# A forward stage whose Haar transform is multiplied into its convolution filters

## The chip, the cores and the metric

The kernel runs on one core of one Trainium2 chip. The metric is device time in microseconds (us) of one execution, as a median of several. Engines are named as in the profile: PE is TensorE's matmul, PEld its weight loads, DVE VectorE, ACT ScalarE, POOL GpSimd, SP SyncE, whose queue issues nearly all DMAs here.

## The reference

Four layers act one after the other on x, float32 of shape (4, 64, 256, 256). Layers 0, 2 and 3 are long convolutions along both image axes with separable filters, plus a bias times the input. Layer 1 goes to 2-D Haar coefficients, mixes channels, shrinks, and goes back.

```python
# layers 0, 2, 3: hx, hy are [256, 64] filters from a small sine network
k = einsum('ijk,imk->ijmk', hx, hy)            # separable, one per channel
y = irfft2(rfft2(x, 512) * rfft2(k, 512) / 512)[:256, :256]   # causal convolution
x = y + x * bias[:, None, None]

# layer 1
f1 = haar2d(x); acc = 0
for i in range(2):
    f4 = einsum('bchw,oc->bohw', f1 * v[i], conv_w[i])
    acc += sign(f4) * relu(abs(f4) - tau[i])
x = haar2d(acc, inverse=True) + x
```

## The kernel before, in words

**Groups and rounds.** The four images form two groups of two. A round is two channels of one group, so each group has 32 rounds, and a round's tile is [128, 8, 256] float32 (1 MB): an image axis is cut into four blocks of 64 rows, and the 128 partitions are two halves of 64.

**Phase A, forward** (`phase_a`, 64 rounds): layer 0 and the forward Haar. A convolution along one axis is a product with a Toeplitz matrix. `load_toeplitz` reads it from DRAM, where each filter was repeated, with a sheared access pattern; `toeplitz` then does 16 matmuls of 64x64 weights for each block row j, four at a time in the four quarters of PE (`TILES`), with 256, 192, 128 and 64 moving columns for k = 0 to 3. The data are the weights, the filter moves, so that each product also transposes. A round has four `rows` pieces (PSUM tiles `a1ps`, emptied by ACT into `ay`, L441) and four `columns` pieces (`a2ps`, emptied by DVE, which adds bias times x in `residual`, L461). The Haar along the free axis is eight levels of sums and differences on POOL (`forward_free`, L341 and L343, 16 instructions a round). The Haar along the other axis is a product with a 64x64 matrix (`product`, PSUM `a3ps`, L305), scaled by row on DVE (L474). `store` writes the coefficients to DRAM (`coef0`, `coef1`).

**Phase B, coefficients** (`phase_b(0)`, `phase_b(1)`, 64 steps for each group): layer 1's middle. A step has two units, one for each i. A unit: mixing on PE (`mix`, L603), times v on DVE (L622), `sign` (L628) and `abs` (L634) on ACT, minus tau (L639) and the thresholded product (L644) on DVE; the sums with the residual's coefficients are POOL's (L659 to L663). `join` on DVE finishes the Haar over the four blocks for the first steps. `abs` writes to PSUM, where it has one buffer. Results go to DRAM (`mixed0`, `mixed1`).

**Phase C, inverse** (`phase_c`, 64 rounds): the inverse Haar on POOL (on DVE for rounds 0 and 1, L384) and PE, then layers 2 and 3 with the same `toeplitz` (`c1r`, `c1c`, `c2r`, `c2c`).

**Order.** All engines run in an order written out by hand. Each phase is a list of pieces (ten for a round of phase A, 18 for one of phase C, three for a unit of phase B), and `beside` interleaves two lists. An operation given to `later` is emitted at the start of the next piece (`flush`). The sequence is: A of group 0; A of group 1 beside B of group 0; the last two rounds of A with the start of C; C of group 0 beside B of group 1; C of group 1. Beside phase B, A's products share a ring of four PSUM tiles, used in pairs (`banks`).

```python
    beside(a[cut_a : -2 * A_PIECES], phase_b(0), 2, 0)
    ...
    main = c_first + a_end[:1] + c[:BLOCKS] + c[mid:C_PIECES] + a_end[1:] + c[BLOCKS:mid] + c[C_PIECES:cut_c]
    beside(main, phase_b(1), len(c_first) + len(a_end) + 2 * BLOCKS, 0)
```

The level buffers of the free-axis Haar (`h2` to `h128`, one buffer each) are shared by the forward and the inverse transform. Group 1 of phase A loads x with one DMA of 1 MB (8 KB a partition), and B of group 0 loads v and tau of both i with one of 1 MB.

## Time and profile before

| | us |
|---|---|
| runs: median of 3 (lowest to highest) | 2605.57 (2600.97 to 2605.86) |
| the profiled execution, own time | 2597.8 |
| its span, first to last instruction | 2595.7 |
| granted TensorE clock, mean over the span | 0.979 |

| stage, by the trace | from, to (us) | PE | DVE | ACT | POOL | DMA share |
|---|---|---|---|---|---|---|
| A of group 0, steady part | 65 to 325 | 99% | 54% | 20% | 87% | 0.73 |
| A of group 1 beside B of group 0, steady part | 520 to 1040 | 82% | 96% | 65% | 91% | 0.94 |
| end of B of group 0 to first product of B of group 1 | 1062 to 1167 | 65% | 47% | 18% | 61% | 0.53 |
| C of group 0 beside B of group 1 | 1235 to 1885 | 95% | 63% | 62% | 66% | 0.87 |
| C of group 1, without its last part | 1885 to 2535 | 99% | 75% | 58% | 91% | 0.65 |

The percentages are busy time over the stage's length. A busy PE is not PE at its peak, since matmuls are pipelined and their ends are modelled. The line number behind L is that of the kernel before; the helper `toeplitz` records all convolutions under L293, so they are told apart by their tiles. Idle time of an engine that is not the bottleneck costs nothing.

### The profile page before, as it was taken

What the parts mean: (1) busy time and instruction counts of PE and PEld (TensorE: products, weight loads), DVE (VectorE), ACT (ScalarE), POOL (GpSimd) and SP (SyncE); (2) the same over time, 40 slices, a digit from 0 to 9 for tenths busy, and PEclk for the clock granted to TensorE, in tenths of its full rate; (3) what the DMA queues carried; (4) which work ended last, traced back from release to release, by engine and by line L of the source; (5) the groups of instructions that cost most, each with busy time, mean ns of one, the idle gap of its engine ahead of it and who ended that gap; (6) DMA issues with size and microseconds to landing.
All of it is one profiled execution on the core that took longest, in us unless ns stands there. A gap on an engine that the chain in (4) does not pass through costs nothing.

```text
span 2595.7 us, 118630 instructions
## 1 busy us (share of the span) xinstructions
PE 2343.0 (90%) x53292; PEld 1915.7 (74%) x53292; DVE 1800.2 (69%) x2049; ACT 1325.6 (51%) x2187; POOL 2025.0 (78%) x2428
## 2 busy tenths in 40 slices
PE   5999999788888888768999999999989999999999
PEld 4887877444444444547777877788889999999998
DVE  2555445799999999646666666666658777777773
ACT  1221112566666666226666665666655655655552
POOL 1898887899999999757657666766679999999991
PEclk8999999899999999979999999999999999999999
DMA  7676897699999999556989888888776666666653
GB/s 209 222 242 231 289 311 281 245 347 317 343 330 328 347 319 335 180 194 214 333 302 315 317 303 302 306 304 311 275 224 203 220 208 215 214 220 207 220 165 113
DMA packets 203678, 685.25 MB, mean 264 GB/s; under 512 B 29289, under 2 KB 30826, under 8 KB 190755
## 3 DMA queue, kind: packets, MB, share of 16 engines
q1 hardware_dynamic: 203171, 677.67, 75.8%
q8 instruction: 418, 6.85, 1.1%
q14 instruction: 89, 0.73, 0.1%
HBM read 427.93 MB, written 249.63 MB: 261 GB/s over the span
## 4 chain that ended last, share of the span: by engine, by line
PE 59%; DVE 13%; DMA 8%; POOL 8%; issue 5%; ACT 3%; SPq 2%; DVEq 0%; ACTq 0%; POOLq 0%
PE c2c L293 10%; PE c2r L293 9%; PE c1c L293 9%; PE c1r L293 9%; PE a1ps L293 6%; PE a2ps L293 5%; PE f L603 4%; PE c0ps L305 4%; DMA v<-in_v 3%; DVE x L622 3%; POOL fw L341 3%; POOL f L343 2%; DVE a L639 2%; DVE m L644 2%; PE a3ps L305 2%
## 5 line engine op out<-in xcount | busy, mean ns | idle before, releaser
L293 PEld LDWEIGHTS a2ps<-toep,ay 64*64 64x64 f32 x8192 | 313.2, 138 | 161.7 <-DVE f L474 85.0
L382 POOL TENSOR_TENSOR i<-i,g 128x16 f32<-128x16 f32 x744 | 398.3, 556 | 27.7 <-ACT g L359 0.6
L293 PE MATMUL a2ps<-toep,ay 64*64 64x128 f32 (+3 forms) x8192 | 360.1, 307 | 50.8 <-DVE f L474 42.4
L603 PE MATMUL f<-ft,mix 64*64 64x512 f32 x2048 | 312.0, 619 | 95.6 <-DVE x L622 80.2
L293 PEld LDWEIGHTS c2c<-toep,ch 64*64 64x64 f32 x8192 | 314.6, 134 | 59.0 <-ACT ch L836 25.9
L293 PEld LDWEIGHTS a1ps<-toep,x 64*64 64x64 f32 x8192 | 293.8, 134 | 83.8 <-issue 43.1
L293 PE MATMUL a1ps<-toep,x 64*64 64x64 f32 (+3 forms) x8192 | 338.8, 300 | 15.3 <-issue 12.3
L293 PEld LDWEIGHTS c1c<-toep,ch 64*64 64x64 f32 x8192 | 313.3, 134 | 51.6 <-ACT ch L836 26.6
L662 POOL TENSOR_TENSOR gt<-m,ft 128x512 f32<-128x512 f32 x128 | 163.6, 1278 | 236.3 <-DVE m L644 230.7
L293 PE MATMUL c1r<-toep,z 64*64 64x128 f32 (+3 forms) x8192 | 324.4, 299 | 21.5 <-issue 11.6
L293 PE MATMUL c2c<-toep,ch 64*64 64x192 f32 (+3 forms) x8192 | 328.7, 300 | 11.8 <-ACT ch L836 8.7
L293 PEld LDWEIGHTS c1r<-toep,z 64*64 64x64 f32 x8192 | 303.9, 134 | 46.6 <-issue 22.2
L293 PE MATMUL c1c<-toep,ch 64*64 64x128 f32 (+3 forms) x8192 | 324.3, 299 | 11.1 <-ACT ch L836 10.4
L382 POOL TENSOR_TENSOR ci<-i,g 128x1024 f32<-128x1024 f32 x124 | 318.2, 2586 | 4.5
L293 PE MATMUL c2r<-toep,cy 64*64 64x128 f32 (+3 forms) x8192 | 318.4, 298 | 2.9 <-issue 2.7
L293 PEld LDWEIGHTS c2r<-toep,cy 64*64 64x64 f32 x8192 | 301.4, 134 | 24.7 <-issue 13.3
L441 ACT COPY ay<-a1ps 128x512 f32<-128x512 f32 x256 | 137.4, 589 | 353.6 <-PE a1ps L293 353.0
L628 ACT ACTIVATE m<-x 128x1024 f32<-128x1024 f32 x194 | 206.3, 1063 | 194.2 <-DVE x L622 87.6
L639 DVE TENSOR_TENSOR a<-a,v 128x1024 f32<-128x1024 f32 x192 | 236.3, 1231 | 49.0 <-ACT a L634 48.9
L836 ACT COPY ch<-c2r 128x512 f32<-128x512 f32 x256 | 137.5, 591 | 247.1 <-PE c2r L293 246.6
L634 ACT ACTIVATE a<-x 128x1024 f32<-128x1024 f32 x194 | 199.6, 1029 | 109.4 <-DVE m L644 109.4
L855 DVE SCALAR_TENSOR_TENSOR cy<-z,bias_sb,c1c 128x512 f32<-128x512 f32 x256 | 176.9, 742 | 109.5 <-PE c1c L293 109.5
(80 smaller groups left out, 3869.2 us busy)
## 6 DMA issues: line engine op xcount, KB each, us to landing
toep<-filt SPq DMA_DIRECT2D x384, 224.0 KB, 5.3
ft<-coef SPq DMA_DIRECT2D x128, 512.0 KB, 7.4
v<-in_v SPq DMA_DIRECT2D x64, 1024.0 KB, 9.4
mixed<-gt SPq DMA_DIRECT2D x128, 512.0 KB, 7.5
g<-mixed SPq DMA_DIRECT2D x256, 256.0 KB, 5.7
x<-in_x SPq DMA_DIRECT2D x128, 256.0 KB, 4.7
coef<-f SPq DMA_DIRECT2D x128, 256.0 KB, 4.2
x<-in_x SPq DMA_DIRECT2D x32, 1024.0 KB, 7.8
```

Of the source, the lines that this page charges most:

```text
L293: nc.tensor.matmul(ps[r][half(c), j % 2, k * ROW :], data[half(r), c, k, bass.ts(j, ROW)], t(r, c)[:, : N - k * ROW], start=k == 0, stop=k ...
L305: nc.tensor.matmul(ps[r][half(c)].rearrange("p h k -> p (h k)"), matrix[half(r)], pairs(r, c).rearrange("p h k -> p (h k)"), start=True, s ...
L341: nc.gpsimd.tensor_tensor(diffs, even, odd, ALU.subtract)
L382: engine.tensor_tensor(to, s, d, op)
L441: later(lambda y=y, ps=ps: nc.scalar.copy(y, ps))
L603: nc.tensor.matmul(un[u]["f4"][half(q), b, :], mixers[0][half(r), bass.ts(i, C)], st[s]["f"][half(r), b], start=True, stop=True, tile_posi ...
L628: nc.scalar.activation(un[u]["m"], un[u]["x"], AF.Sign)
L634: nc.scalar.activation(un[u]["a"], un[u]["x"], AF.Abs)
L639: nc.vector.tensor_tensor(un[u]["a"], un[u]["a"], both(u, "tau"), ALU.subtract)
L662: nc.gpsimd.tensor_tensor(g[:, 0], m[:, 0], st[s]["f"][:, 0], ALU.add)
L836: later(lambda y=y, ps=ps: nc.scalar.copy(y, ps))
L855: nc.vector.scalar_tensor_tensor(to, of, bias_sb[:, at : at + 1], ps, ALU.mult, ALU.add)
```

## The change

It concerns rounds 32 to 63 of phase A, the second group's forward stage.

- `fold` multiplies each round's filters by Haar matrices: `load_hankel` reads the two filters with the opposite shear (2304 B a partition instead of 3584), 32 matmuls of 64x64 by 64 columns form the products, and ACT and DVE copy them to `fold` (one 128x512 copy each). `rows` and `both_axes` then use `fold` in place of the Toeplitz tiles, so their results are already transformed within blocks of 64.
- The bias term becomes a product of its own: `plain` transforms x along one axis (64 matmuls of 64 columns a round, copied by ACT to `u`), and `both_axes` adds `u` times the other Haar matrix times the bias to the same PSUM sum (64 more). DVE's residual and x's long life go.
- `f` comes out of `both_axes` by plain copies, half on ACT, half on DVE. `forward_free`, `product` and the row scaling are not used for these rounds. What is left of the Haar, over the four blocks, is `join_blocks`, five small POOL instructions.
- The end of phase A is shorter: the list `a_end` is gone, and B of group 1 starts four pieces earlier in the main list.
- The second image of the second group comes with its halves swapped, so the mixing has a second, swapped matrix and the inverse Haar writes its PSUM tiles crossed (`haar(..., crossed)`).
- x (group 1) and v with tau (B of group 0) are loaded in two DMAs of 4 KB a partition each. Two buffers of phase B move into a tile of phase A that the second group no longer uses.

```diff
+    def load_hankel(t):
+        rows = ac.tile([P, SPAN - ROW], F32, tag="toep", name=f"hankel_{t}", bufs=4)
+        for r in range(2):
+            start = filt[0].offset + (t % ROUNDS * 2 + r) * REPEATS * SPAN + PERIOD - ROW + 1
+            src = bass.AP(filt[0].tensor, start, [[SPAN + 4, 16], [SPAN + 1, 4], [1, PERIOD + N]])
+            nc.sync.dma_start(rows[half(r), : PERIOD + N], src)
+        return rows
...
-            toeplitz(s["ps"], blocks(s["x"]), filters_x(s["toep"]), j)
+            x_of = (lambda r, c: s["fold"][half(r), c, 0]) if folded(t) else filters_x(s["toep"])
+            toeplitz(s["ps"], blocks(s["x"]), x_of, j)
...
+            if j % 2 and folded(t):
+                plain(t, j)
+
+        def fold(t):
+            s = st[t]
+            s["fold"] = fp.tile([P, 2, 2, N], F32, tag="fold", name=f"fold_{t}", bufs=3)
+            two = banks(f"foldps_{t}")
+            for i in range(2):
+                for k in range(BLOCKS):
+                    for r, c in TILES:
+                        nc.tensor.matmul(
+                            two[r][half(c), i, bass.ts(k, ROW)],
+                            s["hankel"][half(r), i * PERIOD + k * ROW : i * PERIOD + (k + 1) * ROW],
+                            folds_sb[half(r), 0, 0 if i else c], ...
+            def evacuate():
+                nc.scalar.copy(s["fold"][:, 0], two[0])
+                nc.vector.tensor_copy(s["fold"][:, 1], two[1])
+                nc.vector.tensor_scalar(s["bias"], folds_sb[:, 1, 0], pairs_sb[:, at : at + 1], None, ALU.mult)
+            later(evacuate)
+
+        def plain(t, j):
...
+            two = banks(f"u{j}ps_{t}")
+            for i in range(2):
+                for k in range(BLOCKS):
+                    for r, c in TILES:
+                        nc.tensor.matmul(
+                            two[r][half(c), i, bass.ts(k, ROW)],
+                            data[half(r), c, k, bass.ts(j - 1 + i, ROW)],
+                            folds_sb[half(r), 1, r], ...
+            for r, ps in enumerate(two):
+                u = blocks(s["u"])[:, r, j - 1 : j + 1]
+                later(lambda u=u, ps=ps: nc.scalar.copy(u, ps))
+
+        def both_axes(t, j):
...
+            for name in ("y", "u"):
+                data = blocks(s[name])
+                for k in range(BLOCKS):
+                    for r, c in TILES:
+                        q = r ^ c
+                        whole = name == "y"
+                        nc.tensor.matmul(
+                            s["ps2"][c][half(q), j % 2, k * ROW : N if whole else (k + 1) * ROW],
+                            data[half(r), c, k, bass.ts(j, ROW)],
+                            s["fold"][half(r), r, 1, : N - k * ROW] if whole else s["bias"][half(r)], ...
+            if j % 2:
+                for b, ps in enumerate(s["ps2"]):
+                    f = s["f"][:, 2 * (j - 1) + 2 * b : 2 * (j - 1) + 2 * b + 2]
+                    copy = nc.vector.tensor_copy if b else nc.scalar.copy
+                    later(lambda f=f, ps=ps, copy=copy: copy(f, ps))
...
-            if j < middle and 1 < t:
+            if j < half_way and 1 < t <= ROUNDS + 1:
                 run(st[t - 2]["ops"], 3 if j < BLOCKS else 2)
+            if j == 1 and folded(t - 2):
+                join_blocks(t - 2)
+            if j == 3 and folded(t - 2):
+                store(t - 2)
...
-                if 2 < t:
+                if 2 < t <= ROUNDS + 2:
                     product(t - 3, j - BLOCKS)
+                if j == BLOCKS + 1 and folded(t + 1):
+                    fold(t + 1)
...
-    main = c_first + a_end[:1] + c[:BLOCKS] + c[mid:C_PIECES] + a_end[1:] + c[BLOCKS:mid] + c[C_PIECES:cut_c]
-    beside(main, phase_b(1), len(c_first) + len(a_end) + 2 * BLOCKS, 0)
+    main = c_first + c[:BLOCKS] + c[mid:C_PIECES] + c[BLOCKS:mid] + c[C_PIECES:cut_c]
+    beside(main, phase_b(1), len(c_first) + 2 * BLOCKS, 0)
```

## The prediction

> **What bounds the kernel now.** I read the busy time by stage first, because the share of the whole span (PE 90%) mixes stages with different limits. One row per stage; columns: length, then busy time and instructions of PE, PE's weight loads, DVE, ACT and POOL, granted clock, DMA share, GB/s.

> ```profile
> 325.00:448.00 123.00, 111.34 (x2646) 94.75 (x2641) 59.68 (x97) 23.21 (x42) 93.36 (x160) 0.97 0.86 297
> 520.00:1040.00 520.00, 424.93 (x6891) 252.33 (x6887) 496.88 (x508) 337.56 (x419) 472.52 (x518) 0.98 0.94 333
> 1062.00:1167.00 105.00, 68.34 (x1196) 49.83 (x1186) 49.38 (x90) 18.80 (x40) 64.30 (x99) 0.82 0.53 186
> 1235.00:1885.00 650.00, 615.06 (x14104) 518.10 (x14108) 411.54 (x434) 402.29 (x708) 428.53 (x516) 1.00 0.87 306
> ```

> Row 2 is the stage where the second group's forward rounds run beside the first group's coefficient steps: DVE is busy 496.88 of 520 us, 96%. Row 3 is the hand-over to the inverse stage: no engine is full and TensorE's clock falls to 0.82. Row 1 (forward alone) and row 4 are PE's. Next, the groups of instructions in 520 to 1040 us, shapes kept apart (count | busy, mean ns | idle before):

> ```profile
> L639 DVE TENSOR_TENSOR a<-a,v 128x1024 f32<-128x1024 f32 x111 | 136.8, 1233 | 18.4 <-ACT a L634 18.4
> L622 DVE TENSOR_TENSOR x<-f,v 128x1024 f32<-128x1024 f32 x111 | 134.9, 1216 | 0.0
> L644 DVE SCALAR_TENSOR_TENSOR m<-a,m 128x1024 f32<-128x1024 f32 x110 | 134.3, 1221 | 4.8
> L461 DVE SCALAR_TENSOR_TENSOR x<-x,bias_sb,a2ps 128x512 f32<-128x512 f32 x88 | 61.5, 741 | 0.0
> L474 DVE TENSOR_TENSOR f<-a3ps,wrow_sb 128x512 f32<-128x512 f32 x88 | 56.3, 681 | 0.0
> ```

> 88/4 = 22 rounds and 111 units (half steps) fit here: 23.6 us a round, 4.68 us a unit, 5.05 units a round. The last two rows, 117.8 us, are the forward rounds' own; DVE's idle time is only 23 us. Last, the hand-over in order of time, one line each of POOL, DVE and PE:

> ```profile
> 1097.50 1.89 POOL L341 TENSOR_TENSOR fw<-x 128x1024 f32<-128x1024 f32 x1 [11.24 <-DVE x L461]
> 1107.54 0.26 DVE L384 SCALAR_TENSOR_TENSOR i<-g 128x8 f32<-128x8 f32 x2 [10.12 <-POOL fw L343]
> 1108.75 6.60 PE L293 MATMUL a2ps<-toep,ay 64*64 64x256 f32 x128 [10.20 <-DVE f L474]
> ```

> The three wait in a ring: POOL's Haar levels (16 instructions, 10 us a round) wait for DVE's residual, DVE's first inverse Haar waits for POOL (it takes the same level buffers), and PE's next columns wait for DVE.

> [...] The trace lists 133 ns for one such load, but single matmul records at 2100.111, 2100.167 and 2100.225 us, two of them with 64 moving columns, start 56 to 58 ns apart in one pair of tiles: 133 ns is latency [...] Here the two tiles of a pair start 7 ns apart[...] DVE, which empties PSUM, is the full engine.

> **The change, part by part** (all in rounds 32 to 63).

> *DVE.* Removed per round: four residuals (L461) and four row scalings (L474), 117.8/22 = 5.35 us. Added: two copies of f, one of the folded filter (128x512; the inverse stage's DVE copy of that shape takes 692 ns, 44.3 us over 64) and a 64-wide bias scaling (about 0.15 us by the 16- to 32-element rows): 2.2 us. Busy time is 496.88/22 = 22.6 us a round (durations overlap by up to 0.1 us, so the removal is worth slightly less than listed); it becomes about 19.4.

> *ACT.* Four copies of ay stay. Added: four of u, two of f, one of the fold, 7 at 590 ns = 4.1 us a round. 337.56/22 = 15.3 becomes 19.4 us. These copies wait for PE at the head of ACT's queue, and behind them stand `sign` and `abs` of the first group, which DVE waits for.

> *POOL.* The 16 levels leave, (41.7+22.9+13.5+8.8+6.5+5.5+4.9+4.6) us x 2 over 22 rounds = 9.9 us a round. The join of the four blocks adds five instructions of at most 32 elements, about 1.2 us by the 210 to 250 ns rows. POOL falls from 91% to near 55%.

> *PE.* Added per round: 32 (fold) + 64 (plain) + 64 (bias) matmuls of 64 columns = 40 sets of four tiles; each is two records at 56 ns: 4.5 us. Removed: the eight 512-column Haar matmuls, 1.7 us (forward alone: a1ps starts 10.45 us apart, 4.37 + 4.37 + 1.7). Rows and columns 8.7, mixing 5 x 0.9: 14.9 becomes 17.7 us a round. If a weight load could not hide, at 133 ns a record, it would be 23.8. I take 56 ns, which the trace shows. The four PSUM tiles now carry seven pairs a round instead of six, and `a1ps2` may start only once ACT has emptied `a1ps0`, under 0.9 us of plain products: PE's 4 us of slack a round covers such waits unless ACT is late by more than about 1 us four times a round.

> *DMA.* The hankel rows are 2304 B in place of 3584, and 451 packets of 8192 B a round (x and v) become 902 of 4096. In the packet records of this stage 8192 B takes 390 ns, 4096 B 171, 3584 B 178 (2304 B: about 110, estimated from these). DMA's time per engine is 0.944 x 23.6 = 22.3 us a round; it loses 451 x 48/16 = 1.35 us and 128 x 68/16 = 0.55 us: 20.4. It can be less if packets meet less traffic, or nothing is saved if 4096 B packets slow to 195 ns. SP issues one DMA more for each step and each round, 0.35 to 0.7 us each, on a queue that mostly waits for buffers; x is now freed by PE, not by DVE's residual, which SP waited 107 us for.

> *The pace beside the first group's steps.* Floors are now DVE 19.4, ACT 19.4, PE 17.7, DMA 20.4 us: balanced, with two lumps. Twice a round four copies (2.2 us) stand on ACT between one `abs` and the next, where `sign` and every other time `exchange` (1.25 us) also stand; a unit of 3.9 us leaves 2.8 us there, so about 1.5 us a round comes back as waits of DVE's L639 for ACT. I take 21.6 us a round, 4.28 us a unit. Some 118 of the 128 units are in the steady part: 118 x 0.40 = **47 us less** (DVE's floor at today's 96%: 4.0 us, 80 less; bound above by no gain).

> *Before it.* At the end of forward alone PE sets the pace. Up to the cut at round 34, piece 8, it gains four folds (32 sets), three plains (48) and half of three bias products (24): 104 sets x 0.112 = **11 us more**. DVE and ACT are idle there, so copies hide.

> *Hand-over.* 1062 (last threshold of the first group) to 1166.9 us (first product of the second) is 105 us. After: rows and columns left are 5 x 4.37 = 21.9 us, small products 88 sets = 9.9 us, so forward ends 32 us after the last threshold. Copies and join 3, two stores landing 9 to 10, loads of ft landing 7, join on DVE 6 to 12, first mix 2: about 65 us. The inverse Haar of rounds 0 and 1 on DVE no longer meets POOL, and the PE work that stands between (four c1/c0 batches, some 17 us) fits under these latencies. **40 us less** (20 to 50: g and v loads of 8 to 10 us stay in the same SP queue).

> *Later.* The second group's swapped images cost nothing: the crossed Haar writes one PSUM bank from two row groups, as the mixing does today (eight records in 0.91 us, the same as the Haar's 0.86 within 6%); the second mixer is 32 KB more in one load.

> Sum on the profiled execution, 2597.8 us (span 2595.7 and 2.1 around it): 2597.8 + 11 - 47 - 40 = 2522. The median of the runs is 2605.57, 7.8 us above it; I add 6: **2528 us**. For this likeliest case alone, 2490 to 2565.

> **Rivals.**
> 1. *ACT or DMA takes DVE's place.* Both come to 19 to 20 us a round; if queueing eats the rest, the stage stays at 23.6 us: 2597.8 + 11 - 40 + 6 = 2575. For: DMA share already 0.94. Against: DVE's idle list shows no wait for DMA.
> 2. *The waits were all DVE's.* 20.2 us a round: 2597.8 + 11 - 80 - 45 + 6 = 2490.
> 3. *Slower: weight loads bind PE.* Runs of 16 to 64 small matmuls do not occur now; only two records of 64 columns follow each other. If in a run each record of a pair costs the listed 133 ns, PE needs 23.8 us a round, near 25 at 95% efficiency: +31 us; forward alone +28; hand-over only -25: 2597.8 + 34 + 6 = 2638. The sign turns at about 118 ns a record. Against: the loads have to follow each other at 56 ns in the pair seen.

> That the Haar does not leave POOL and DVE is excluded by the order of instructions built: L461 and L474 have no counterpart for rounds 32 to 63.

> **Chances.** Likeliest 0.46, rival 1 0.17, rival 2 0.16, rival 3 0.18, near no change 0.03. About 0.2% is what a measurement of this kernel can tell from no change. Faster 0.79, same 0.03, slower 0.18. The range 2475 to 2612 leaves out most of rival 3 and the low half of rival 2.

> **What the profile after would show.** DVE's rows f<-a2ps at 690 ns, 64 in number, and no L461 for these rounds; units 4.2 to 4.4 us apart; waits of DVE for ACT's abs growing from 18 to 30-60 us; POOL near 55%; 64-column matmul sets 112 ns apart; first product of the second group some 65 us after the first group's last threshold. If the sets stand over 200 ns apart, or units stay at 4.7 us, the prediction is wrong in the step named PE, or ACT and DMA.

## The result and the profile after

The kernel after takes 2693.61 us (median of 4 runs, 2679.85 to 2700.62), the kernel before 2603.27 us in the same comparison (2596.94 to 2605.86): a ratio of 1.034, 95% interval 1.030 to 1.039. The change makes the kernel slower; the forecast was 2528 us.

Marks in the two traces divide the spans (us; B(0) and B(1) are phase B of group 0 and 1, and a mark is DVE's first product with v or its last thresholding of a group):

| | to the first product of B(0) | B(0) | hand-over | B(1) | rest | span | one unit of B(0) |
|---|---|---|---|---|---|---|---|
| before | 443.2 | 618.8 | 104.9 | 715.1 | 713.7 | 2595.7 | 4.72 |
| after | 480.5 | 695.8 | 80.8 | 714.8 | 719.7 | 2691.5 | 5.50 |
| difference | +37 | +77 | -24 | 0 | +6 | +96 | +0.78 |

The hand-over shrinks, as forecast. Everything is lost in the second group's forward rounds, most of it beside B(0), where 47 us were to be won. The stages of the kernel after, in the form in which the prediction showed those of before (length, busy time and instructions of PE, PEld, DVE, ACT, POOL, granted clock, DMA share, GB/s); rows: forward alone, beside B(0), hand-over, beside B(1):

```profile
325.00:483.00 158.00, 129.66 (x3800) 114.74 (x3796) 56.24 (x97) 33.80 (x63) 72.56 (x135) 0.96 0.70 239
560.00:1160.00 600.00, 450.47 (x13553) 372.71 (x13549) 432.51 (x418) 410.67 (x572) 289.78 (x275) 0.95 0.81 282
1176.00:1257.00 81.00, 66.77 (x1926) 56.43 (x1930) 30.48 (x63) 27.63 (x57) 25.68 (x51) 0.94 0.59 206
1330.00:1960.00 630.00, 596.59 (x13683) 499.87 (x13678) 399.61 (x421) 390.32 (x684) 415.52 (x499) 1.00 0.88 307
```

In row 2 no engine is full: PE 75%, DVE 72% (it was 96%), ACT 68%, POOL 48%, and DMA fell from 0.94 to 0.81. PE alone also falls from 91% to 82% in row 1. A stage in which everything is idle part of the time waits for something that has no column here. The waits of the kernel after from 600 to 1100 us (engine and line, what it waited for: us in total, times, longest) say where to look:

```profile
DVE products L745 <- PE f L723: 118.7, 58, 7.1
PEld a2ps L531 <- issue: 58.8, 83, 3.5
ACT f L543 <- PE a2ps L531: 49.5, 21, 5.4
PEld a1ps L310 <- issue: 39.9, 57, 3.9
PEld u1ps L506 <- issue: 24.1, 8, 4.6
PEld foldps L478 <- issue: 23.9, 34, 3.1
```

DVE waits for PE's mixing (118.7 us; this wait was not in the list of before), ACT waits for PE's columns, and PE waits for "issue", which is time in which the profile shows nothing that it waits for. POOL's long waits, left out here, are for DVE and follow from the first line. So PE is the late one, and PE is not waiting for data. The chain of work from 838 to 850 us shows the form of it (start, length, what):

```profile
838.32 1.10 PE u1ps L506 x60
...
841.43 0.96 PE a1ps L310 x22
842.39 3.52 issue
845.90 0.28 PE a1ps L310 x4
...
846.24 0.88 PE u3ps L506 x60
...
848.02 0.71 PE foldps L478 x46
848.73 2.92 issue
```

A batch of `a1ps` products stops in the middle for 3.5 us, and a fold for 2.9 us. Between the stops the small products run fast: 60 records of `u1ps` in 1.10 us, the last one's own 0.2 us included. From 560 to 1160 us each of the four tiles starts its next record of a `u1ps`, `u3ps` or `foldps` batch 58 to 59 ns after the last (median), where the prediction priced 56 ns. Now the DMA queues, first on the page of before, then on that of after (packets, MB, share):

```profile
q8 instruction: 418, 6.85, 1.1%
```

```profile
q8 instruction: 495, 8.11, 1.3%
```

Instructions come by DMA: these lines count 6.85 and 8.11 MB of them. In the packet records those of q8 have 16,384 B each. The 495 packets of the kernel after stand against 126,040 records of PE and PEld, the 418 of before against 106,584, so 255 records for each packet. One packet is thus 128 weight loads and 128 matmul records, or 64 products of these float32 matmuls: each of them is two weight loads and two records (in the stage from 520 to 1040 us of before, 22 rounds of 156 products have 6887 loads and 6891 records). In the stop at 842 us the last weight load starts at 842.06, a q8 packet runs from 843.57 to 844.53, and PE goes on at 845.90. This is no single case: from 560 to 1160 us PE has 60 stops of over 0.9 us that end within 1.8 us of such a packet's landing (median 1.37 us after it), 154 us together; of the 59 stretches between two such stops, 53 hold a multiple of 128 weight loads, to within 3. A wait for data has no reason to fall on such counts. Here a piece of `plain` happens to be 128 loads too, but in e2 below, where a piece has 80, all stretches hold such a multiple. **PE runs out of instructions.** The small products (64 columns) double the number of instructions of a round but not its columns, and the instructions arrive one packet every 5.6 us in this stage (9.6 us in that of before, where PE needs fewer). This interval is counted over the stage, so it says how many packets PE used and not how fast they could have come; the stops say that it waited for them.

The counts also show how far the packets run ahead of PE. In the kernel after, 128 loads for each packet begun, less the loads started, taken whenever a packet begins, is a difference that moves by under 160 loads within any stretch of 150 us, so the supply never gets more than about one packet ahead of PE.

### The profile page after: what moved, and what is told of

Read it like the earlier page. It is cut to its first block, busy times and chain, and to the rows that moved or that the text cites. A ratio compares the mean times of both kernels' runs of the same rounds, so it can differ in the third digit from the quotient of the medians.

```text
span 2691.5 us, 138172 instructions
## 1 busy us (share of the span) xinstructions
PE 2390.1 (89%) x63020; PEld 2069.6 (77%) x63020; DVE 1717.1 (64%) x1921; ACT 1434.9 (53%) x2411; POOL 1759.1 (65%) x2076
## 3 DMA queue, kind: packets, MB, share of 16 engines
q8 instruction: 495, 8.11, 1.3%
## 4 chain that ended last, share of the span: by engine, by line
PE 73%; issue 9%; DVE 8%; ACT 4%; DMA 3%; SPq 1%; POOL 1%; DVEq 0%; ACTq 0%; POOLq 0%
PE a1ps L310 10%; PE c2c L310 9%; PE c2r L310 9%; PE c1r L310 8%; PE c1c L310 8%; PE f L723 8%; PE a2ps L531 7%; PE a2ps L310 5%; PE c0ps L322 3%; PE a3ps L322 2%; DVE x L907 2%; PE foldps L478 1%; PE u3ps L506 1%; PE u1ps L506 1%; DVE o L984 1%
## 5 line engine op out<-in xcount | busy, mean ns | idle before, releaser
L310 PEld LDWEIGHTS c1c<-toep,ch 64*64 64x64 f32 x8192 | 314.6, 135 | 56.3 <-ACT ch L965 29.7
L310 PE MATMUL c2c<-toep,ch 64*64 64x128 f32 (+3 forms) x8192 | 332.6, 300 | 16.5 <-ACT ch L965 9.1
L723 PE MATMUL f<-ft,mix 64*64 64x512 f32 x2048 | 322.1, 618 | 19.2 <-issue 5.2
L310 PE MATMUL c1r<-toep,z 64*64 64x256 f32 (+3 forms) x8192 | 321.5, 298 | 8.6 <-issue 6.9
L310 PEld LDWEIGHTS c2r<-toep,cy 64*64 64x64 f32 x8192 | 296.7, 133 | 27.0 <-issue 14.9
L965 ACT COPY ch<-c1r 128x512 f32<-128x512 f32 x256 | 137.7, 592 | 210.3 <-PE c1r L310 209.7
L785 POOL TENSOR_TENSOR gt<-gt,m 128x1024 f32<-128x1024 f32 x66 | 156.3, 2368 | 142.2 <-DVE m L767 122.4
L310 PEld LDWEIGHTS a1ps<-fold,x 64*64 64x64 f32 x4096 | 184.5, 142 | 78.6 <-issue 52.2
L984 DVE SCALAR_TENSOR_TENSOR o<-cy,bias_sb,c2c 128x512 f32<-128x512 f32 x256 | 176.9, 743 | 106.6 <-PE c2c L310 106.6
L767 DVE SCALAR_TENSOR_TENSOR m<-a,m 128x1024 f32<-128x1024 f32 x194 | 236.9, 1221 | 10.2
L310 PE MATMUL a1ps<-fold,x 64*64 64x192 f32 (+3 forms) x4096 | 198.7, 315 | 41.6 <-issue 31.2
L531 PEld LDWEIGHTS a2ps<-fold,ay 64*64 64x64 f32 x4096 | 177.8, 138 | 73.2 <-issue 57.9
```

The source lines that it names most:

```text
L310: nc.tensor.matmul(ps[r][half(c), j % 2, k * ROW :], data[half(r), c, k, bass.ts(j, ROW)], t(r, c)[:, : N - k * ROW], start=k == 0, stop=k ...
L531: nc.tensor.matmul(s["ps2"][c][half(q), j % 2, k * ROW : N if whole else (k + 1) * ROW], data[half(r), c, k, bass.ts(j, ROW)], s["fold"][h ...
L723: nc.tensor.matmul(un[u]["f4"][half(q), b, :], mixers[0][half(r), b * grp, bass.ts(i, C)], st[s]["f"][half(r), b], start=True, stop=True, ...
L767: nc.vector.scalar_tensor_tensor(un[u]["m"], un[u]["a"], 0.0, un[u]["m"], ALU.max, ALU.mult)
L785: nc.gpsimd.tensor_tensor(st[s]["g"], st[s]["g"], m, ALU.add)
L965: later(lambda y=y, ps=ps: nc.scalar.copy(y, ps))
```

## The experiments

Theory F: PE is short of instructions in stretches of many small products. The expectations put on record before each run set it against theory W (small products or their weight loads are slow to execute) and theory P (PE waits until ACT has emptied PSUM). For each kernel the table gives the products of a round beside B(0) (mixing included), one unit of B(0), PE's pauses from 600 to 950 us (over 0.6 us, ended by a q8 packet, ahead of products of phase A; mixing is left out, since it waits for DVE too; by how the ends of a pause are taken, a sum moves by some 10 us), the mean interval of q8 packets there, the hand-over, and the ratio to the kernel before. Times are in us.

| | products | unit | pauses of 350 | interval | hand-over | ratio (95% interval) |
|---|---|---|---|---|---|---|
| before | 156 | 4.72 | 10 | 9.7 | 105 | 1 |
| after | 308 | 5.50 | 86 | 5.7 | 81 | 1.034 (1.030 to 1.039) |
| e1_wide | 228 | 4.44 | 24 | 6.2 | 74 | 0.979 (0.972 to 0.986) |
| e2_split | 348 | 5.91 | 107 | 5.5 | 123 | 1.081 (1.078 to 1.084) |
| e3_quiet | 308 | 4.63 | 39 | 4.8 | 83 | 1.003 (1.002 to 1.005) |
| e4_rows8k | 308 | 5.47 | 80 | 5.6 | 81 | 1.033 (1.030 to 1.036) |
| e5_joined | 244 | 4.84 | 31 | 6.3 | 77 | 1.005 (1.003 to 1.006) |
| e6_nobias | 180 | 4.04 | 0 | 7.2 | 70 | 0.954 (0.953 to 0.956) |
| e7_before4k | 156 | 4.72 | 10 | 9.6 | 105 | 0.999 (0.997 to 1.000) |
| e8_half_split | 252 | 5.16 | 80 | 6.7 | 112 | 1.033 (1.031 to 1.036) |
| e9_alternate | 244 | 4.88 | 19 | 6.4 | 87 | 1.011 (1.009 to 1.014) |
| e10_half_alt | 252 | 5.03 | 56 | 6.5 | 114 | 1.026 (1.022 to 1.030) |
| e11_tail | 156 | 4.72 | 12 | 9.7 | 82 | 0.992 (0.990 to 0.994) |

**e1_wide**: the same small products, half as many and twice as wide.

```diff
-                for k in range(BLOCKS):
+                for k in range(0, BLOCKS, 2):
                     for r, c in TILES:
                         nc.tensor.matmul(
-                            two[r][half(c), i, bass.ts(k, ROW)],
+                            two[r][half(c), i, k * ROW : (k + 2) * ROW],
...
-                            folds_sb[half(r), 0, 0 if i else c],
+                            folds_sb[half(r), 0].rearrange("p a b -> p (a b)"),
```

> The changed kernel with its small matmuls (fold, plain, bias) halved in number and doubled in width: 80 of 128 columns a round instead of 160 of 64. The columns streamed, the PSUM tiles and all copies stay; the values of these products are not those of the reference. Theory F (PE starves for instructions: they arrive in packets of 256, about 5.6 us apart while PE waits): 456 weight loads a round instead of 616, 3.6 packets instead of 4.8, 20 us, so other engines set the pace again: a unit of phase B falls from 5.50 to 4.3 to 4.5 us and the profiled execution from 2693 to about 2560. Theory W (small matmuls or their weight loads are slow to execute) and theory P (PE waits for ACT to empty PSUM): the same columns and copies, so a unit stays at 5.3 to 5.5 us and the total within 25 us of 2693.

Measured: 2543.91 us (2 runs), a unit of 4.44 us. The columns of PE are unchanged, the instructions fewer, and the loss turns into a gain. This alone does not rule out theory W, as its expectation has it: half as many small products also halve whatever each of them costs. Against theory W speaks the pace of 58 to 59 ns above, which is that of the price.

**e2_split**: the kernel before, with group 1's wide products cut to 64 columns; nothing of the Haar is folded.

```diff
+        if cut:
+            sets = [(k, n, n + ROW) for n in range(0, N, ROW) for k in range(n // ROW + 1)]
...
-            toeplitz(s["ps"], blocks(s["x"]), filters_x(s["toep"]), j)
+            toeplitz(s["ps"], blocks(s["x"]), filters_x(s["toep"]), j, t >= ROUNDS)
```

> The kernel before, with the second group's forward products cut into pieces of 64 moving columns: 320 matmuls a round for 128, the same columns streamed, the same values, nothing else changed. Theory F: 696 weight loads a round instead of 312, 5.4 packets of instructions, about 30 us at 5.6 us a packet: a unit of phase B goes from 4.72 to about 6 us and the total from 2600 to 2750 to 2800. Theory W: PE gains weight loads but hides them as now; if a set of four small tiles costs 112 ns a record pair, PE's work grows by under 0.5 us a round and the total stays within 15 us; if each costs over 200 ns, about +6 us a round and a total like F's, but without PE standing still until an instruction packet has landed. Theory P: no change, PSUM tiles and copies are the same.

Measured: 2809.48 us (2 runs), a unit of 5.91 us. More instructions for the same values, columns and copies make the loss, more than twice over. The cut products too start 58 to 59 ns apart in a tile, so it is not their execution. The granted clock is lower in this kernel (0.85 from 600 to 950 us, against 0.99 before); what that adds was not separated. Its waits from 600 to 1000 us hold the same line, now of both products:

```profile
PEld a1ps L297 <- issue: 88.7, 79, 5.2
...
PEld a2ps L297 <- issue: 64.8, 84, 4.9
```

Here all 62 stretches between two stops (560 to 1200 us) hold a multiple of 128 weight loads, though a piece has 80.

**e3_quiet**: the kernel after, without most of B(0)'s loads of v and tau.

```diff
             d = st[s]
+            if grp == 0 and s >= 3:
+                d["v"], d["tau"] = kept[s % 3]
+                return
             d["v"], d["tau"] = [], []
+            kept.append((d["v"], d["tau"]))
```

> The changed kernel without the loads of v and tau for the first group's steps 3 to 63 (they reuse those of steps 0 to 2, so the coefficients differ from the reference's). Instructions of PE, DVE and ACT are the same; DMA moves some 60 MB less in that stage. Theory F with the packets of instructions held up by the data on the DMA engines: packets come at 4.5 us or less instead of 5.6, a unit falls to 4.3 to 4.6 us, total 2560 to 2600. Theory F with a fetch time of its own, whatever the traffic: a unit stays near 5.4 us. Theories W and P: 5.4 to 5.5 us too.

Measured: 2602.13 us, a unit of 4.63 us, DMA share 0.64 in place of 0.81. With the same instructions on PE, DVE, ACT and POOL the packets come 4.8 us apart instead of 5.7, and the pauses fall from 86 to 39 us. Waits for the loads of v themselves are not what fell away: from 600 to 1100 us they were 3.9 us in the kernel after. So the traffic of the data delays the instructions, and the traces show where. Between two stops that are 128 loads apart (500 to 1250 us, means), a packet begins 3.6 us after PE has gone on in the kernel after and 2.7 us in e3; its own record takes 1.0 us in both, and PE goes on 1.4 us after its end in both. The delay lies ahead of the packet's record.

**e4_rows8k**: the kernel after with x (group 1) and v in rows of 8 KB again, and **e7_before4k**: the kernel before with rows of 4 KB.

```diff
-        n = CI if grp == 0 else M
+        n = CI if grp == 0 else 2 * M
...
-            fetch(0, 1, "v")
-            if not raw(2 * s + 1):
+            fetch(0, 2 if grp < GROUPS - 1 else 1, "v")
+            if grp == GROUPS - 1 and not raw(2 * s + 1):
                 fetch(1, 1, "raw")
```

> The changed kernel with x (second group) and v with tau (first group's steps) again in one DMA each of 8 KB rows. Prediction's DMA step: 48 ns more for each 8 KB, not the bound: within 15 us of 2693. Theory F with traffic: an instruction packet waits behind longer data packets, 5.6 becomes 5.6 to 6.0 us: a unit of 5.5 to 5.9 us, total 2693 to 2745. If rows of 4 KB were what made the stage slow (twice the packets): a unit under 5.0 us.

> The kernel before with only the rows of x (group 1) and v at 4 KB, nothing else changed. Theory F, with the result that 8 KB rows in the kernel after made no difference: within 0.3% of the kernel before. Rival, smaller rows bring x and v in earlier and are a gain of their own, or cost issues on SP: a change of 10 us or more either way.

Measured: e4 2685.79 us (2 runs), within the range of the kernel after's own runs; e7 2597.73 us, 0.15% below the kernel before in the same comparison (interval 0.03% to 0.28%), as theory F expected (e7's edit is the reverse of the one shown). This part of the change is worth a few us at most. In e4 the instruction packets come 5.6 us apart, as in the kernel after (5.7), so the number of packets of x and v is not what delays them.

**e6_nobias**: the kernel after without the bias term's 128 small products a round.

```diff
-            if j % 2 and folded(t):
-                plain(t, j)
...
-            for name in ("y", "u"):
+            for name in ("y",):
```

> The kernel after, without the bias term of group 1: no plain products, and none of the 64 products of the bias in both_axes, so its coefficients lack that term. 180 products a round are left, 360 weight loads. Theory F: 2.8 packets, 16 us for a round, no limit; the stage goes at the pace of the next thing, DVE (19.4 us) and the DMA queues (20.4 us): a unit of 4.2 to 4.4 us, 2500 to 2550 us in all. Rival, the longer chain through ACT's copies and PSUM sets the pace: the chain of fold, rows and columns is as before, so a unit stays over 4.7 us and the kernel over 2600 us.

Measured: 2483.49 us, faster than the forecast range, and a unit of 4.04 us. The stretch from 600 to 950 us, first of the kernel after, then of e6 (columns as above):

```profile
600.00:950.00 350.00, 264.86 (x7984) 217.91 (x7975) 255.19 (x247) 241.54 (x337) 169.58 (x162) 0.95 0.81 280
```

```profile
600.00:950.00 350.00, 269.31 (x6228) 187.12 (x6220) 336.77 (x330) 287.75 (x383) 228.34 (x221) 1.00 1.01 384
```

(The four copies of u a round are gone with them; ACT was not full in either kernel.) DVE is back at 96% and the DMA engines are full; which of the two sets the pace was not separated. A round is 5.05 x 4.04 = 20.4 us: the world that the prediction described, with its DVE at 19.4 and its DMA at 20.4 us, is what this kernel shows, and the bias products are what keeps the kernel after out of it.

**e8_half_split**: e2 with the cut in `rows` only.

```diff
-            toeplitz(s["ps2"], blocks(s["y"]), filters_y(s["toep"]), j, t >= ROUNDS)
+            toeplitz(s["ps2"], blocks(s["y"]), filters_y(s["toep"]), j)
```

> The kernel before, with only the first product (rows) of group 1 cut to pieces of 64 columns; the second product (columns) keeps its wide pieces. Values are those of the kernel before. A round then has 252 products, so 504 weight loads. Theory F (PE is fed 256 instructions, 128 weight loads and 128 products, at a time, every 5.6 us beside B(0)): 3.9 packets, 22 us for a round, still under the 23.8 us that a round takes: a unit stays at 4.7 to 4.9 us and the kernel within 1% of the one before (2597 to 2625 us). Rival, each added small product costs PE its own time: half of what cutting both products cost, a unit near 5.3 us and the kernel near 2700 us.

Measured: 2688.03 us, a unit of 5.16 us. This missed the expectation of theory F, which counted instructions over a round: 3.9 packets a round were to fit (its "128 products" for a packet are 128 matmul records). The numbers of the rival, 5.3 and 2700 us, came closer, but its mechanism, a cost of each product, is not what the trace shows. The waits from 600 to 1000 us show why an average does not do:

```profile
PEld a1ps L297 <- issue: 96.2, 90, 5.9
...
PEld a2ps L297 <- issue: 23.5, 87, 0.6
```

The long pauses stand in the cut product (longest 5.9 us); those of the wide one are 0.3 us on average. What is short in the four pieces of `rows` is not made up by the plenty in the others, since the packets run no more than about one ahead of PE (under 160 loads in the kernel after).

**e10_half_alt**: the products of e8, with pieces of `rows` and `columns` in turn; and **e9_alternate**, the same of e5 (below), with the fold over two pieces and smaller copies of f.

```diff
-            if j < BLOCKS:
+            if ROUNDS <= t < total and not BLOCKS <= j < half_way:
+                i = j if j < BLOCKS else j - 2
+                if i % 2:
+                    columns(t - 1, i // 2)
+                else:
+                    rows(t, i // 2)
+            elif j < BLOCKS:
```

> The kernel of e8_half_split with the same products in another order: in group 1 a piece of rows (40 small products) alternates with a piece of columns (16 wide ones). Values are those of the kernel before. Theory F with bursts: 504 weight loads a round, 3.9 packets, 22 to 24 us when spread evenly: a unit of 4.7 to 4.95 us and 2600 to 2650 us. Rival, only the number in a round counts: a unit of 5.1 to 5.2 us and 2680 to 2700 us, as e8_half_split.

> The kernel of e5_joined with the same products in another order: in group 1 the pieces of rows and columns alternate (rows 0, columns 0, rows 1, columns 1, fold, fold, ...), the fold is cut over two pieces, and the coefficients are evacuated after each block, 256 columns at a time in place of 512. Values are those of the kernel after. Theory F with bursts (PE keeps little in store, so small products that stand close together starve it while wide ones elsewhere do not pay back): 488 weight loads a round, now spread evenly, 21 to 23 us at 5.6 to 6 us for 128: a unit of 4.4 to 4.65 us, 2550 to 2590 us in all. Rival, only the number in a round counts: a unit of 4.8 us and 2600 to 2620 us, as e5_joined, or more for the smaller evacuations.

Measured: e10 2662.55 us, a unit of 5.03 us, pauses 56 us in place of 80. Spreading the small products helps, which a cost of each product can't explain, since their number is the same. The gain is a third to two thirds of what was expected. In this order PE also waits for copies, from 600 to 1000 us:

```profile
PEld a1ps L297 <- ACT ay L445: 25.2, 22, 3.4
PEld a1ps L297 <- DVE f L478: 22.9, 26, 1.5
```

Neither wait is in the list of e8. So the refinement is right in its sign, and this run does not tell its size. e9 2628.22 us against 2610.40 of e5: pauses fall from 31 to 19 us and the kernel gets slower all the same; this is taken up under e5.

**e5_joined**: `plain` joined to `rows`. Both load the same piece of x, so one product with a moving tile of filter and Haar block side by side gives y and u.

```diff
+                    nc.tensor.matmul(
+                        two[r][half(c), :, k * ROW :],
+                        data[half(r), c, k, bass.ts(j, ROW)],
+                        s["fold"][half(r), c : c + 2, : N - k * ROW],
+                        start=k == 0,
+                        stop=k == BLOCKS - 1,
...
-            if j % 2 and folded(t):
-                plain(t, j)
```

> The kernel after, with plain joined to rows: both load the same 64x64 piece of x, so the moving tile is laid out as the filter beside a 64x64 Haar block with zeros behind it, and one product of up to 512 columns gives y and u. The values are those of the kernel after. 244 products a round in place of 308, 488 weight loads, and 2.7 us more of columns on PE. Theory F: 3.8 packets, 21 us for a round, against 27 us for after: a unit of 4.4 to 4.7 us, and the kernel at 2540 to 2600 us, level with the one before or faster. Rival, PE's own time counts: the columns added eat what the products removed save, a unit of 5.2 us or more and the kernel over 2650 us.

Measured: 2610.40 us (22 runs), a unit of 4.84 us: most of the loss of the kernel after is gone with a fifth fewer products, but the unit is above the range that theory F gave. Its stage and that of e9, in this order:

```profile
600.00:950.00 350.00, 315.08 (x7111) 246.48 (x7106) 285.31 (x292) 271.56 (x395) 190.61 (x179) 0.97 0.90 322
```

```profile
600.00:950.00 350.00, 315.54 (x7013) 238.92 (x7009) 281.00 (x316) 272.13 (x416) 189.04 (x183) 0.99 0.88 313
```

PE is busy 315 of 350 us in both, and with the pauses of 31 us in e5 that is nearly all of the time. The zeros behind the Haar block make 1280 columns for each block row in place of 640 + 256, so in e5 PE's own work is near the limit as well. It is not why fewer pauses in e9 bought nothing: PE's busy time did not grow there. In their place PE waits for copies of ACT, from 600 to 1000 us above all for this one:

```profile
PEld a1ps L522 <- ACT u L532: 11.9, 18, 2.5
```

With the copies of ay and of the fold these waits come to 28 us, against 5 us for the like in e5, and DVE's wait for the mixing rose from 48.8 to 73.1 us. e9 changed the order, the fold and the size of the copies of f (and with them takes the PSUM ring twice as often for `columns`) at once; which of them brought the waits was not taken apart.

**e11_tail**: the joined form for the last three rounds only; the other 29 rounds of group 1 stay as before.

```diff
-            return ROUNDS <= t < total
+            return total - 3 <= t < total
...
-            haar(two, lambda r, c: fw[half(r), c, 2 * bp : 2 * bp + 2], forward_sb)
+            haar(two, lambda r, c: fw[half(r), c, 2 * bp : 2 * bp + 2], forward_sb, turned=t >= ROUNDS)
```

> The joined form of e5_joined, but only for the last three rounds of group 1; the other 29 rounds have the toeplitz products, the residual, the free Haar transform and product of the kernel before (their Haar product is turned, so that the coefficients lie as the folded ones do). Values are those of the kernel after. Theory F: the rounds beside B(0) keep the 312 weight loads of the kernel before, so nothing starves: the stretch to the first product of B(0) stays at 440 to 450 us and a unit at 4.7 us, while the hand-over falls from 105 to the 75 to 85 us that every folded kernel showed: 2565 to 2590 us. Rival, the shorter hand-over of the folded kernels comes only because their stage B(0) ran slower and the forward stage had got ahead of it: the hand-over stays near 100 us and the kernel at 2590 to 2605 us.

Measured: 2578.04 us (6 runs), faster than both kernels, 0.8% below the one before. Its rows for the steady stage and the hand-over:

```profile
520.00:1040.00 520.00, 422.53 (x6864) 251.66 (x6868) 497.03 (x509) 336.70 (x420) 471.66 (x518) 0.98 0.95 334
1066.00:1148.00 82.00, 70.67 (x1630) 51.85 (x1624) 37.23 (x75) 26.90 (x56) 34.50 (x63) 0.96 0.67 241
```

The first row is that of the kernel before to about 1%, the second is 82 us long in place of 105. The shorter hand-over does not come from a slower B(0), which is 623.5 us here and 618.8 before. It comes with the folded form, but e11 also keeps the shorter order at the end of phase A (no `a_end`, B of group 1 four pieces earlier); no run has one without the other, so how much is due to each is not shown.

## Why the prediction was wrong

- **PE, the step that failed.** It priced 40 sets of four small tiles by what they take to execute, 112 ns each, and that price was right to 5%: at 58 to 59 ns a record in each tile a set takes 117 ns. It left out that each product is also four instructions (two weight loads, two matmul records, by the counts above) that have to reach PE: 308 products a round in place of 156, 4.8 packets in place of 2.4. At 5.6 us a packet 4.8 packets take 27 us; the round took 5.05 x 5.50 = 27.8 us. (Both are counted in the same stage, so they agree in any case; that PE waited for the packets is shown by the stops and by e1, e2, e3 and e6.) The floor of 17.7 us a round for PE, and the 4 us of slack that the prediction counted on, were of columns and not of instructions.
- **Rival 3** had the sign and the engine, by another mechanism. It wanted 133 ns for each record of a tile, the time that the trace of before lists for one 64x64 weight load; they come 58 to 59 ns apart, then stop. It gave 2638 us and was too low by 56.
- **DVE and ACT.** Right. DVE's row scaling and residual are gone, the copies of f take 684 ns, and DVE needs 336.77/350 x 20.4 = 19.6 us a round in e6 (19.4 forecast). ACT needs 241.54/350 x 27.8 = 19.2 us in the kernel after (19.4).
- **DMA.** The floor of 20.4 us is the round of e6, where the share is 1.01. In the kernel after it is 0.81 x 27.8 = 22.5 us, the 22.3 of before and not less: the saving of the 4 KB rows did not come there. Its packets of 4096 B took 189 ns on average from 600 to 950 us, near the 195 ns at which the prediction saw nothing saved (171 in the kernel before, 170 in e6). e4 and e7 show that little hung on it.
- **Pace beside B(0).** Forecast 4.28 us a unit, 4.04 once the bias products are out, 5.50 with them. Whether the 1.5 us a round for lumps on ACT was too much is not shown: DVE's wait for `abs` was 8.5 us in 500 us in the kernel after, not 30 to 60, but there DVE was late for another reason, and e6 lacks the four copies of u that made up the lumps.
- **Before B(0).** Forecast +11, measured +37. Pauses of PE from 325 to 480 us come to 25 us (7 us in that stretch of the kernel before); without the bias products, in e6, it is +6.
- **Hand-over.** Forecast -40, measured -24; -35 in e6. The ring of POOL, DVE and PE that the prediction read out of this stage cannot form without its L341, L461 and L474, and all folded kernels have the shorter hand-over, e11 among them; what the shorter order of pieces adds is open. That the rest of the difference is starvation too is likely, since the hand-over of the kernel after has pauses of 6.5 us, but was not taken apart.
- **Later.** Right: B(1) 714.8 against 715.1 us, the rest 6 us longer, as in kernels without swapped images too (e2 719.8, e7 717.4, against 713.7 before).

What stays open is what sets the interval of the packets. It was 4.8 to 6.7 us in starved stages, the shortest tenth under 3.7 us in the kernel after. Data traffic is a part of it (e3) and the packets run little ahead of PE (under 160 loads by the counts above; e8 fits that). The packet's own record takes 1.0 us of a cycle of 6.0; what fills the 3.6 us before it is not in the records, nor is the moment when the packet is asked for.

## What to carry to other kernels

Count instructions as well as columns: before splitting matmuls into small ones, count the PE records (weight loads and matmuls) of the densest stretch in blocks of 256 (here a packet had 255 by the counts), and compare the time that PE needs to execute a block with the interval of the q8 packets at that DMA load (here 4.8 to 6.7 us where PE was short of them); an average over a round hides the shortage (e8: 3.9 packets a round were to fit, and it took 2688.03 us). When PE stops with "issue" as the cause, at regular counts, and q8 packets land just before it goes on, fewer and wider products (e1, e5) or less traffic (e3) helped here (2543.91, 2610.40 and 2602.13 us in place of 2693.61). Reordering gained 1% once (e10 against e8) and lost 0.7% once (e9 against e5), as it brought waits of its own. A change that is right for a latency-bound stretch and wrong for a full one can be made in the first alone, as e11 does (2578.04 us).
